# Adding the shared part of a routed feed-forward block onto scattered rows by accumulating stores

## The chip, the cores and the metric

The kernel runs on one core of a Trainium2 chip. The metric is device time in microseconds (us). Engine names are those of the profile: PE multiplies matrices (PEld is its weight load), DVE, ACT and POOL work on tiles, SP only issues transfers. PE writes to banks of PSUM; everything else lives in on-chip tiles or in device memory (names that end in `_dram`, the inputs `in_...`, and the result `out`).

## The reference

For 4096 tokens (2 sequences of 2048) of width 256, in 32-bit floats, the result is a sum of four parts:

```python
xn  = layernorm(x)
out = x + attention(xn) + (xn + moe(layernorm(xn, ln_w, ln_b)))
```

`attention` is a causal linear attention with 16 heads of 16 channels: queries and keys are expanded into Chebyshev polynomials up to order 5, prefix sums run over the tokens, and a numerator is divided by a denominator before the output projection. `moe` is the feed-forward block:

```python
logits  = xf @ router_w                       # 8 experts
top_idx = argmax(logits); top_score = sigmoid(max(logits))
routed  = for each token, with expert e = top_idx and xe = xf * top_score:
              (silu(xe @ gate_w[e]) * (xe @ up_w[e])) @ down_w[e]
shared  = (silu(xf @ sh_gate) * (xf @ sh_up)) @ sh_down
moe     = routed + shared
```

Each token goes to exactly one expert, so each row of the result gets exactly one routed row.

## The kernel before

The 4096 tokens are cut into 8 chunks of 512 tokens (`NC`, index `c`), each of 4 tiles of 128 rows (`NT`, index `t`). One on-chip tile per chunk, `X[c]` with 128 partitions x 4 x 256, first holds the input rows, then `x + xn`, and then takes the results of the attention and of the shared experts by additions on DVE: `accumulate` (L958) adds two row tiles at a time from a PSUM bank; for the very last pair, chunk 7's tiles 2 and 3, L949 adds one tile at a time.

Routed experts work on sorted tokens. `route` computes for 34 slot tiles (`NJ`) of 128 rows which token sits in which row: `take_i` and `give_i`. `expert(n, j)` loads the weights of the expert of slot tile `j` on SP's queue, gathers its 128 rows by an indirect transfer on POOL's queue (L1183), multiplies (L1201 for gate and up, L1222 for down), copies the result from PSUM to a tile `yt` (L1225 on ACT or L1226 on DVE), and scatters `yt` by an indirect transfer on POOL's queue (L1229) to the rows `give_i` of the scratch tensor `y_dram`; padding rows have an index out of bounds and are left out. Each scatter is recorded in `y_ins`.

When all 34 scatters have landed, the last loop of the kernel (L1247 on) combines the two halves. For each chunk SP loads 512 KB of `y_dram` into a free weight buffer (L1251; the load has explicit dependencies on all instructions in `y_ins`), DVE adds it to `X[c]` (L1260, one instruction over 128 x 1024), and SP stores `X[c]` to the result (L1264): one transfer of 512 KB per chunk, but for the last chunk 256 KB and twice 128 KB.

The order of instructions on each engine is computed when the program is built: `op` declares an operation with its engine, an assumed cost, what it reads (`r`), writes (`w`) and adds to (`a`), and a priority; `Plan.order` simulates the engines and emits operations as they become ready. The numbers in `op` (0.45, 1.25 and so on) are this planner's assumptions. Each engine then runs its own list in order, and waits on semaphores where data come from elsewhere. The shared experts' last two chunks are held back (`hold`) so that PE computes them at the end, beside and behind the last routed tiles. Combining has the lowest priority (`60 + c`), so it stands last on every queue that it uses.

Of the kernel before, what the change touches and what calls it, by code (L numbers as in the profile page):

```python
# [11 lines left out]
F32 = mybir.dt.float32  # L12
I32 = mybir.dt.int32
AF = mybir.ActivationFunctionType
ALU = mybir.AluOpType
# [3 lines left out]
SP = mybir.EngineType.SP  # L19

P = 128
NB, S, D = 2, 2048, 256
NTOK = NB * S
NH, DH = 16, 16
NE, FF = 8, 512
CH = 512
NT = CH // P
# [11 lines left out]
NJ = NFULL + (NPART + 3) // 4  # L39
# [60 lines left out]
class Plan:  # L100
# [13 lines left out]
    def op(self, eng, cost, emit, r=(), w=(), a=(), prio=0.0, alloc=(), nbytes=None, alt=(), table=None,  # L114
           after=(), grow=None):

        o = Op()
        o.seq, o.prio, o.alloc, o.nbytes, o.table, o.grow = len(self.ops), prio, list(alloc), nbytes, table, grow  # L120
        o.alts = [(eng, cost, emit)] + list(alt)
        need = {}
        for k in r:
            need.update(dict.fromkeys(self.adds.get(k, ())))
            if k in self.last:
                need[self.last[k]] = None
            self.reads.setdefault(k, []).append(o)
        for k in a:
            if k in self.last:
                need[self.last[k]] = None  # L130
            need.update(dict.fromkeys(self.reads.get(k, ())))
            self.adds.setdefault(k, []).append(o)
        for k in w:
            if k in self.last:
                need[self.last[k]] = None
            need.update(dict.fromkeys(self.reads.get(k, ())))
            need.update(dict.fromkeys(self.adds.get(k, ())))
            self.last[k], self.reads[k], self.adds[k] = o, [], []
        need.pop(o, None)
        o.soon = [n for n in after if n not in need]  # L140
        need.update(dict.fromkeys(after))
        o.need, o.after, o.done = need, [], None
        o.bufs = {}
        for k in tuple(r) + tuple(w) + tuple(a):
            b = k[0] if isinstance(k, tuple) else k
            if isinstance(b, Buf):
                o.bufs[b] = None
        for b in o.alloc:
            b.owner = o
        for b in o.bufs:  # L150
            b.users += 1
            if b.owner is not o:
                need[b.owner] = None
        self.ops.append(o)
        return o
# [100 lines left out]
def kernel(  # L256
# [19 lines left out]
    dram = ctx.enter_context(tc.tile_pool(name="dram", bufs=1, space=DRAM))  # L276
# [2 lines left out]
    ctx.enter_context(tc.manual_schedule())  # L279

    z_dram = dram.tile([NTOK, D], F32, name="z_dram")
    y_dram = dram.tile([NTOK, D], F32, name="y_dram")
    ratio_dram = dram.tile([NTT, P], F32, name="ratio_dram")
    xn_dram = [dram.tile([P, KD, CH], F32, name=f"xn_dram_{c}") for c in range(NC)]
    xf_dram = [dram.tile([P, KD, CH], F32, name=f"xf_dram_{c}") for c in range(NC)]
# [37 lines left out]
    give_i = const.tile([P, NJ], I32, name="give_i")  # L323
# [3 lines left out]
    X = [const.tile([P, NT, D], F32, name=f"X_{c}") for c in range(NC)]  # L327
# [27 lines left out]
    w_p = Pool([big[:, i * 1024 : (i + 1) * 1024] for i in range(NW)])  # L355
# [15 lines left out]
    op = plan.op  # L371
    V, A, G, S_, T_ = nc.vector, nc.scalar, nc.gpsimd, nc.sync, nc.tensor
    MM, M256, MT = 0.86, 0.442, 0.115
    KiB = 1024
# [13 lines left out]
    for c in range(NC):  # L388
        if c == 0:
            for t in range(NT):  # L390
                op("SP", 0.45, lambda t=t: S_.dma_start(out=X[0][:, t, :], in_=x[ts(t, P)]),
                   w=[("X", 0, t)], nbytes=128 * KiB, prio=-90)
# [7 lines left out]
                out=rw[:, :, NE * (GP - 1) : NE * GP], in_=router_w.rearrange("(k p) e -> p k e", p=P)), w=["rw"], nbytes=64 * KiB, prio=-88.5)  # L400
            op("SP", 0.45, lambda: S_.dma_start(out=sg, in_=sh_gate.rearrange("(k p) f -> p k f", p=P)),
               w=["sg"], nbytes=512 * KiB, prio=-88)
            op("SP", 0.45, lambda: S_.dma_start(out=su, in_=sh_up.rearrange("(k p) f -> p k f", p=P)),
               w=["su"], nbytes=512 * KiB, prio=-87)
        else:
            op("SP", 0.45, lambda c=c: S_.dma_start(
                out=X[c], in_=x[c * CH : (c + 1) * CH].rearrange("(t p) d -> p t d", p=P)),
               w=[("X", c, t) for t in range(NT)] + [("x_in", c)], nbytes=512 * KiB, prio=-80 + 5 * c)
        if c == 1:
            op("SP", 0.45, lambda: S_.dma_start(out=sd, in_=sh_down.rearrange("(k p) d -> p k d", p=P)),  # L410
               w=["sd"], nbytes=512 * KiB, prio=-73)
            op("SP", 0.45, lambda: S_.dma_start(out=w_in, in_=w_in_t.rearrange("(k p) e -> p k e", p=P)),
               w=["w_in"], nbytes=768 * KiB, prio=-74)
        if c == 2:
            op("SP", 0.45, lambda: S_.dma_start(out=w_out, in_=w_out_t.rearrange("(k p) e -> p k e", p=P)),
               w=["w_out"], nbytes=256 * KiB, prio=-68)
# [18 lines left out]
    def stat(c, tiles=range(NT), behind=()):  # L435
        for t in tiles:
            i = c * NT + t

            def f(c=c, t=t, i=i):
                V.bn_stats(stats[:, i, :], X[c][:, t, :])  # L440
                V.bn_aggr(mv[:, i, :], stats[:, i, :])

            op("DVE", 0.58, f, r=[("X", c, t)], w=[("mv", i)], prio=FRONT + 0.1 * c - 0.15,
               after=evicted + list(behind))
# [50 lines left out]
    def front(c):  # L495
# [7 lines left out]
        for t in range(NT):  # L503
            i = c * NT + t

            def f(t=t, i=i):
                V.tensor_scalar(zall[:, i, :], X[c][:, t, :], mv[:, i, 0:1], rs[:, 1, i : i + 1],
                                ALU.subtract, ALU.mult)

            def f_(t=t, i=i):  # L510
                A.activation(zall[:, i, :], X[c][:, t, :], AF.Identity,
                             bias=nm[:, 2, i : i + 1], scale=rs[:, 1, i : i + 1])
            if c:
                op("ACT", 0.59, f_, r=[("X", c, t), ("r", part(c, t)), ("nm", part(c, t))], w=[("z", i)], prio=p,
                   alt=[("DVE", 0.36, f)])
            else:
                op("DVE", 0.36, f, r=[("X", c, t), ("r", part(c, t))], w=[("z", i)], prio=p - 0.37 + 0.1 * (t // HT))
# [107 lines left out]
    for cs in ([0], [1], [2, 3], [4, 5, 6, 7]):  # L625
# [4 lines left out]
        else:  # L630
            for c in cs:
                stat(c)
            a, b = cs[0] * NT, (cs[-1] + 1) * NT
# [502 lines left out]
    for g in range(KD):  # L1136
        b = Buf(T_p, f"W_{g}")
# [5 lines left out]
    for i in range(2):  # L1143
        b = Buf(xfT_p, f"V_{i}")
# [3 lines left out]
    for i, (q, n) in enumerate(((zt_p, D), (sl_p, FF), (hm_p, FF), (yt_p, D))):  # L1148
        b = Buf(tv_p, f"U_{i}")
# [5 lines left out]
    y_ins, downs, ups = [], [], []  # L1155

    def expert(n, j):
# [15 lines left out]
        for n, src, cost in ((0, gate_w, 0.85), (1, up_w, 0.45), (2, down_w, 0.45)):  # L1173
            for i, (h, _) in enumerate(parts):
                def f(h=h, i=i, n=n, src=src, b=sets[i][n]):
                    if n == 0:
                        ev.append(nc.values_load(expert_i[0:1, h : h + 1], engines=[SP], min_val=0, max_val=NE - 1))
                    S_.dma_start(out=b.t.rearrange("p (k f) -> p k f", k=KF if n == 2 else KD),
                                 in_=src[ds(ev[i], 1)].rearrange("o (k p) f -> p (o k) f", p=P))
                downs.append(op("SP", cost, f, r=["experts"] + [("z_dram", n) for n in range(NC)], w=[sets[i][n]],  # L1180
                                alloc=[sets[i][n]], nbytes=512 * KiB, prio=EXQ + e, after=downs[-1:]))

        op("POOL", 1.28, lambda: G.indirect_dma_start(  # L1183
            out=zt.t, out_offset=None, in_=z_dram,
# [4 lines left out]
        def f():  # L1189
            for k in range(KD):  # L1190
                T_.transpose(pz.t[:, ts(k, P)], zt.t[:, ts(k, P)], ident)  # L1191
        op("PE", 2 * MT, f, r=[zt], w=[pz], alloc=[pz, xT], prio=EXQ + e)
        for k in range(KD):
            op("ACT", 0.46, lambda k=k: A.activation(
# [3 lines left out]
        def mm(b, wts_):  # L1198
# [9 lines left out]
           prio=EXQ, table="silu")  # L1208
        op("DVE", 0.75, lambda: V.scalar_tensor_tensor(sl.t, pu.t, sc(), sl.t, ALU.mult, ALU.mult),  # L1209
           r=[pu, zt, sl], w=[sl], prio=EXQ)  # L1210
# [16 lines left out]

        def f():
            y_ins.append(G.indirect_dma_start(  # L1229
                out=y_dram, out_offset=bass.IndirectOffsetOnAxis(ap=give_i[:, j : j + 1], axis=0),  # L1230
                in_=yt.t, in_offset=None, bounds_check=NTOK - 1, oob_is_err=False,
            ).ins)
        op("POOL", 1.28, f, r=[yt, "table"], w=[("y", j)], nbytes=128 * KiB, prio=SCAT)
# [10 lines left out]
        gate = [shared(c, gate + ([hold[c]] if c in hold else spilled if c > 1 else []))]  # L1244


    for c in range(NC):  # L1247
        b = Buf(w_p, f"y_{c}")

        def f(c=c, b=b):  # L1250
            ins = S_.dma_start(  # L1251
                out=b.t.rearrange("p (t d) -> p t d", t=NT),
                in_=y_dram[c * CH : (c + 1) * CH].rearrange("(t p) d -> p t d", p=P),
            ).ins
            for s in y_ins:
                tc.add_manual_dep(ins, s.name, mybir.DependencyInfo(
                    mybir.DependencyClass.Sync, mybir.DependencyReason.DATA))
        op("SP", 0.45, f, r=[("y", j) for j in range(NJ)], w=[b], alloc=[b], nbytes=512 * KiB, prio=60 + c)
        keys = [("X", c, t) for t in range(NT)]
        op("DVE", 1.25, lambda c=c, b=b: V.tensor_tensor(  # L1260
            X[c].rearrange("p t d -> p (t d)"), X[c].rearrange("p t d -> p (t d)"), b.t, ALU.add),
           r=[b], a=keys, prio=60 + c)
        for t, n in ((0, 2), (2, 1), (3, 1)) if c == NC - 1 else ((0, NT),):
            op("SP", 0.45, lambda c=c, t=t, n=n: S_.dma_start(  # L1264
                out=out[ds(c * CH + t * P, n * P)].rearrange("(t p) d -> p t d", p=P), in_=X[c][:, t : t + n, :]),
               r=keys[t : t + n], w=[("out", c, t)], nbytes=n * 128 * KiB, prio=60 + c)

    for _, _, emit in plan.order():
        emit()
# [37 lines left out]
```

## Time and profile before

| | us |
|---|---|
| median of 3 runs (570.54 to 570.64) | 570.56 |
| profiled execution | 570.69 |
| its span, first to last instruction | 569.0 |
| PE busy | 563.1 (99%) |
| DVE busy | 486.2 (85%) |
| ACT busy | 238.0 (42%) |
| POOL busy | 99.7 (18%) |
| eight adds L1260, mean of one | 1.22 |
| two adds L949, mean of one | 0.42 |

The granted clock of TensorE is full throughout. DMA moved 132.67 MB in the span, a mean of 233 GB/s: 121.65 MB by SP's (hardware) queue, 10.51 MB by POOL's (software) queue. The profile's rows name a line, an engine, an operation and the tiles written and read (`out<-in`); "POOLq" and "SPq" stand for what those engines' sequencers do, such as issuing a transfer. The busy time of an issuing row is the time of issue, not that of the data. Buffers are named by the memory they were cut from: the loads of `y_dram` appear as `T<-y_dram`, `big<-y_dram` and `xfT<-y_dram`. The DMA share in a table by stage is the mean busy share of the 16 DMA engines; it can come out a little over 1.

### The profile page before, as it was taken

The page shows a single profiled execution, that of the slowest core. Times are in us where ns is not written, and L with a number is a line of the kernel's source. Part 1 is how long each engine was busy: PE and PEld are TensorE (multiplying, and loading weights), DVE is VectorE, ACT ScalarE, POOL GpSimd, SP SyncE. Part 2 cuts the span into 40 slices and gives each one's busy share as a digit, 9 for nine tenths or more (in the row PEclk, how much of TensorE's full clock was granted, in tenths as well). Part 3 has the DMA queues.
Part 4 walks back from the last instruction along what each step waited for, and adds up shares of the span by engine and source line. Part 5 has one row for each costly group of instructions (what it writes and reads, how often), then busy time and mean ns, then how long its engine had stood idle before and what let it go on. Part 6 is the DMA issues. An engine that isn't in the chain of part 4 may idle for free.

```text
span 569.0 us, 8176 instructions
## 1 busy us (share of the span) xinstructions
PE 563.1 (99%) x2691; PEld 305.4 (54%) x2691; DVE 486.2 (85%) x799; ACT 238.0 (42%) x469; POOL 99.7 (18%) x113
## 2 busy tenths in 40 slices
PE   8999999999999999999999999999999999999997
PEld 7564555665535555464445455464555644553655
DVE  6899899999999999999899998999999999931254
ACT  4779662012553362354236435424733543311110
POOL 4211000005021102212120322215031321210100
PEclk9999999999999999999999999999999999999999
DMA  8857651336249918893884699299679938991089
GB/s 283 275 164 259 223 222 37 126 123 243 74 141 365 333 47 268 304 352 93 297 288 165 219 348 363 53 353 336 234 224 308 388 106 285 380 373 67 10 271 328
DMA packets 87689, 132.67 MB, mean 233 GB/s; under 512 B 5681, under 2 KB 52063, under 8 KB 87648
## 3 DMA queue, kind: packets, MB, share of 16 engines
q1 hardware_dynamic: 83152, 121.65, 62.7%
q0 software_dynamic: 3952, 10.51, 5.3%
q8 instruction: 21, 0.34, 0.3%
q14 instruction: 20, 0.16, 0.1%
q10 hardware_dynamic: 544, 0.00, 0.1%
HBM read 113.26 MB, written 19.15 MB: 233 GB/s over the span
## 4 chain that ended last, share of the span: by engine, by line
PE 98%; DVE 1%; DMA 0%; ACT 0%; issue 0%; DVEq 0%
PE bank L1201 22%; PE bank L924 20%; PE bank L987 15%; PE bank L1222 11%; PE bank L942 10%; PE bank L1125 5%; PE bank L1214 3%; PE psk L1017 3%; PE psq L1017 3%; PE bank L1191 1%; PE psk L1030 1%; PE bank L554 1%; PE psk L1111 1%; PE bank L874 1%; PE bank L587 1%; PE bank L1098 0%
## 5 line engine op out<-in xcount | busy, mean ns | idle before, releaser
L1201 PE MATMUL bank<-big,wide 128*32 128x512 f32 (+1 forms) x344 | 102.9, 596 | 0.0
L1229 POOL DMA_INDIRECT y_dram<-wide,give_i x32 | 41.4, 1293 | 304.1 <-ACT wide L1225 152.1
L987 PE MATMUL bank<-xnT,w_in 128*128 128x512 f32 x192 | 86.7, 594 | 0.0
L1054 DVE TENSOR_TENSOR_SCAN tv<-ones,carry,tv 128x512 f32<-128x512 f32 x60 | 76.6, 1277 | 1.2
L924 PE MATMUL bank<-xfT,sg 128*128 128x512 f32 (+1 forms) x136 | 61.1, 574 | 1.1 <-ACT xfT L532 1.1
L924 PE MATMUL bank<-xfT,su 128*128 128x512 f32 (+1 forms) x136 | 61.0, 573 | 0.0
L1201 PEld LDWEIGHTS bank<-big,wide 128*32 128x32 f32 (+1 forms) x344 | 34.6, 144 | 45.9 <-issue 42.1
L1183 POOL DMA_INDIRECT wide<-z_dram,take_i x34 | 42.9, 1262 | 85.5 <-DVE give_i L899 72.6
L942 PE MATMUL bank<-sd,hT 128*128 128x256 f32 x256 | 57.5, 379 | 0.0
L987 PEld LDWEIGHTS bank<-xnT,w_in 128*128 128x128 f32 x192 | 35.6, 190 | 39.0 <-issue 35.9
L1222 PE MATMUL bank<-big,wide 128*32 128x256 f32 (+1 forms) x352 | 54.2, 384 | 0.0
L942 PEld LDWEIGHTS bank<-sd,hT 128*128 128x128 f32 x256 | 48.0, 190 | 8.7 <-issue 2.5
L931 ACT ACTIVATE hT<-bank 128x512 f32<-128x512 f32 x32 | 19.0, 596 | 77.7 <-PE bank L924 73.5
L1222 PEld LDWEIGHTS bank<-big,wide 128*32 128x32 f32 (+1 forms) x352 | 37.0, 148 | 19.6 <-issue 7.5
L1207 ACT ACTIVATE wide<-bank,slot_s 128x512 f32<-128x512 f32 x33 | 22.6, 686 | 58.7 <-PE bank L1201 58.6
L1201 PE MATMUL bank<-xfT,wide 128*32 128x512 f32 (+1 forms) x100 | 45.6, 597 | 0.0
L1074 DVE TENSOR_TENSOR o<-o,tv 128x512 f32<-128x512 f32 x64 | 44.2, 690 | 1.7
L1209 DVE SCALAR_TENSOR_TENSOR wide<-bank,slot_s,wide 128x512 f32<-128x512 f32 x33 | 24.5, 743 | 17.9 <-PE bank L1201 17.5
L924 PEld LDWEIGHTS bank<-xfT,sg 128*128 128x128 f32 x136 | 24.6, 190 | 26.8 <-issue 24.1
L924 PEld LDWEIGHTS bank<-xfT,su 128*128 128x128 f32 x136 | 24.6, 190 | 25.3 <-issue 23.8
L1009 DVE SCALAR_TENSOR_TENSOR T<-T 128x1024 f32<-128x1024 f32 x32 | 38.1, 1220 | 0.0
L958 DVE TENSOR_TENSOR X<-X,bank 128x512 f32<-128x512 f32 x31 | 21.1, 679 | 15.6 <-PE bank L942 9.3
(224 smaller groups left out, 859.2 us busy)
## 6 DMA issues: line engine op xcount, KB each, us to landing
big<-in_gate_w SPq DMA_DIRECT2D x45, 512.0 KB
big<-in_down_w SPq DMA_DIRECT2D x44, 512.0 KB
big<-in_up_w SPq DMA_DIRECT2D x41, 512.0 KB
xfT<-in_up_w SPq DMA_DIRECT2D x14, 512.0 KB
xfT<-in_gate_w SPq DMA_DIRECT2D x11, 512.0 KB
xfT<-in_down_w SPq DMA_DIRECT2D x9, 512.0 KB
z_dram<-big SPq DMA_DIRECT2D x8, 512.0 KB
X<-in_x SPq DMA_DIRECT2D x7, 512.0 KB
```

Source lines behind the costliest of these rows:

```text
L924: T_.matmul(b.t[:, cols], wt[:, k, ts(f, P)], vx(k)[:, cols], start=(k == 0), stop=(k == KD - 1))
L942: T_.matmul(po.t[:, ts(i, D)], hT[f].t[:, ts(tp * 2 + i, P)], sd[:, f, :], start=(f == 0), stop=(f == KF - 1))
L987: T_.matmul(pm.t, w_in[:, k, ds(i * D + g * P, P)], xnT.t[:, ts(k, CH)], start=(k == 0), stop=(k == KD - 1))
L1009: op("DVE", 1.27, lambda i=i, j=j, q=part: V.scalar_tensor_tensor(q[i](), q[j](), off[i], q[1](), ALU.subtract, ALU.mult), r=[(T, j)] + X2 ...
L1017: T_.matmul(pt.t[ts(i - 1, QD), :], heads[:, 24 - g * HB : 24 - g * HB + QD], half[i](side), start=(g == 0), stop=(g == KD - 1 and (i > KD ...
L1054: o_ = op("DVE", 1.25, lambda b=b, i=i, g=g: V.tensor_tensor_scan(b.t, ones[:, 0:1].to_broadcast([P, CH]), b.t, 0.0 if opening else old[:, ...
L1074: op("DVE", 0.66, lambda o=o, b=b: V.tensor_tensor(o(), o(), b.t, ALU.add), r=[b, ok], w=[ok], prio=p)
L1125: T_.matmul(pa.t[:, ts(i, D)], o2.t[:, ds(g * CH + (tp * 2 + i) * P, P)], w_out[:, g, :], start=(g == 0), stop=(g == KD - 1))
L1183: op("POOL", 1.28, lambda: G.indirect_dma_start(out=zt.t, out_offset=None, in_=z_dram, in_offset=bass.IndirectOffsetOnAxis(ap=take_i[:, j ...
L1201: T_.matmul(b.t[n, :], xT.t[:, ds(k * P + n.start, n.stop - n.start)], wt.t[:, ts(k, FF)], start=(k == 0), stop=(k == KD - 1), skip_group_ ...
L1222: T_.matmul(py.t[n, :D], hmT.t[:, ds(i * P + n.start, n.stop - n.start)], wd.t[:, ts(i, D)], start=(i == 0), stop=(i == KF - 1), skip_grou ...
L1229: y_ins.append(G.indirect_dma_start(out=y_dram, out_offset=bass.IndirectOffsetOnAxis(ap=give_i[:, j : j + 1], axis=0), in_=yt.t, in_offset ...
```

## The change

The scratch tensor `y_dram` goes. The 34 scatters write the routed rows to the result `out` itself. The loads of `y_dram` on SP and the adds on DVE are gone. The ten stores of `X[c]`, with the same sizes as before, are issued from POOL's queue as accumulating stores: what is in `X[c]` is added to what stands in `out`. Each has explicit dependencies on all 34 scatters. The planner gives them an assumed cost of 1.0 on POOL. The order on PE and ACT stays the same instruction by instruction, and DVE's list differs by the eight adds alone.

```diff
-    y_dram = dram.tile([NTOK, D], F32, name="y_dram")
...
             y_ins.append(G.indirect_dma_start(
-                out=y_dram, out_offset=bass.IndirectOffsetOnAxis(ap=give_i[:, j : j + 1], axis=0),
+                out=out, out_offset=bass.IndirectOffsetOnAxis(ap=give_i[:, j : j + 1], axis=0),
                 in_=yt.t, in_offset=None, bounds_check=NTOK - 1, oob_is_err=False,
             ).ins)
...
     for c in range(NC):
-        b = Buf(w_p, f"y_{c}")
-
-        def f(c=c, b=b):
-            ins = S_.dma_start(
-                out=b.t.rearrange("p (t d) -> p t d", t=NT),
-                in_=y_dram[c * CH : (c + 1) * CH].rearrange("(t p) d -> p t d", p=P),
-            ).ins
-            for s in y_ins:
-                tc.add_manual_dep(ins, s.name, mybir.DependencyInfo(
-                    mybir.DependencyClass.Sync, mybir.DependencyReason.DATA))
-        op("SP", 0.45, f, r=[("y", j) for j in range(NJ)], w=[b], alloc=[b], nbytes=512 * KiB, prio=60 + c)
         keys = [("X", c, t) for t in range(NT)]
-        op("DVE", 1.25, lambda c=c, b=b: V.tensor_tensor(
-            X[c].rearrange("p t d -> p (t d)"), X[c].rearrange("p t d -> p (t d)"), b.t, ALU.add),
-           r=[b], a=keys, prio=60 + c)
         for t, n in ((0, 2), (2, 1), (3, 1)) if c == NC - 1 else ((0, NT),):
-            op("SP", 0.45, lambda c=c, t=t, n=n: S_.dma_start(
-                out=out[ds(c * CH + t * P, n * P)].rearrange("(t p) d -> p t d", p=P), in_=X[c][:, t : t + n, :]),
-               r=keys[t : t + n], w=[("out", c, t)], nbytes=n * 128 * KiB, prio=60 + c)
+            def f(c=c, t=t, n=n):
+                ins = G.dma_start(
+                    out=out[ds(c * CH + t * P, n * P)].rearrange("(t p) d -> p t d", p=P), in_=X[c][:, t : t + n, :],
+                    accum_op=ALU.add).ins
+                for y in y_ins:
+                    tc.add_manual_dep(ins, y.name, mybir.DependencyInfo(
+                        mybir.DependencyClass.Sync, mybir.DependencyReason.DATA))
+            op("POOL", 1.0, f, r=keys[t : t + n] + [("y", j) for j in range(NJ)], w=[("out", c, t)], nbytes=n * 128 * KiB,
+               prio=60 + c)
```

## The prediction

> **What bounds the kernel now.** I began with the page's shares: PE is busy 563.1 of 569.0 us at full granted clock, and the chain that ended last is 98% PE. PE's work is untouched by this change, and so is its order, so the question is the stretch behind PE's last matmul, and whatever could push it out. The end of that chain, in order of time (start, length, what):
>
> ```profile
> 544.66 13.73 PE bank L924 x32
> 558.40 6.92 PE bank L942 x32
> 565.32 0.02 issue
> 565.34 0.42 DVE X L949
> 565.76 0.33 DVEq L1303
> ```
>
> PE runs without a gap to 565.32; then DVE adds the last two row tiles (L949), and 2.9 us after that the span is over. The timeline of those us, all engines and then SP's queue from 520 us on:
>
> ```profile
> 565.34 0.75 DVE L949 TENSOR_TENSOR X<-X,bank 128x256 f32<-128x256 f32 x2 [2.77 <-PE bank L942]
> 565.79 0.83 SPq L1264 DMA_DIRECT2D out<-X  x2
> ...
> 542.57 1.47 SPq L1251 DMA_DIRECT2D T<-y_dram  x3
> ```
>
> SP issues each of the last two 128 KB stores in 0.83 / 2 = 0.42 us, as soon as its tile is added (565.76 and 566.09). The eight loads of y start at 542.57, when the last scatter has landed. Line L1303, the end of the program, says that SP is through with its last waits at 568.1; so 0.9 us of the span is the closing barrier:
>
> ```profile
> L1303 SPq DRAIN  x3: 7/7/7, 568.1 to 568.4; - x3
> ```
>
> The third view is the table by stage over the tail (window, length, busy time of PE, PEld, DVE, ACT, POOL, then clock, DMA share, GB/s):
>
> ```profile
> 552.00:554.00 2.00, 2.00 (x6) 0.82 (x5) 2.00 (x3) 0.60 (x1) 0.00 (x0) 1.00 1.10 349
> ...
> 560.00:562.00 2.00, 2.00 (x11) 1.77 (x10) 0.44 (x2) 0.00 (x0) 0.00 (x0) 1.00 1.09 385
> ...
> 565.00:566.00 1.00, 0.30 (x2) 0.00 (x0) 0.66 (x2) 0.00 (x0) 0.00 (x0) 1.00 1.09 384
> 566.00:567.00 1.00, 0.00 (x0) 0.00 (x0) 0.10 (x1) 0.00 (x0) 0.00 (x0) 1.00 0.72 248
> 567.00:568.00 1.00, 0.00 (x0) 0.00 (x0) 0.00 (x0) 0.00 (x0) 0.00 (x0) 1.00 0.45 149
> ```
>
> This is what the shares hide: from 544 to 566 us the DMA engines are full. They move 348 GB/s while loads of y and stores of X are mixed, 385 GB/s when stores are alone. After 566 us 0.248 + 0.149 = 0.40 MB are left, of which the last two stores are 0.26; so the last stores stand behind 0.14 MB, 0.35 us. PE and the DMA engines finish almost together: a tail with little slack in it.
>
> **The change, part by part.**
>
> *Removed, worth about nothing.* Eight adds of 128x1024 (L1260, 1.22 us each, 9.8 us of DVE). From 500 us on DVE is busy 23.6 of 69 us; the adds that matter for the end (L958 at 561.89, L949 at 565.34) start when PE releases them, with DVE waiting 1.56 and 2.77 us. Cover: PE. Eight loads of y (4.19 MB) and SP's issue of them: SP has nothing else to issue there.
>
> *The scatters* go to the result instead of a scratch tensor: the same 34, with the same waits in the same places of POOL's queue, 128 KB each. Nothing.
>
> *Moved and added: ten accumulating stores on POOL's queue*, behind the last scatter and waiting for all 34. Nothing but themselves is queued behind them, and no other engine waits for POOL any more. They can start where the loads of y started, at 542.6; tiles 0 to 6 are complete at 544.70 + 0.69 = 545.4, before their turn. So seven stores of 512 KB and one of 256 KB (its tiles are ready at 561.89 + 0.69 = 562.6) have until 566 us behind PE, and the last two of 128 KB don't.
>
> *POOL's issue.* The trace has no accumulating store. POOL's nearest rows:
>
> ```profile
> L499 POOL DMA_DIRECT2D wide<-ratio_dram x7 | 3.8, 549 | 9.7 <-DMA ratio_dram<-wide 9.7
> L1229 POOL DMA_INDIRECT y_dram<-tv,give_i x2 | 2.0, 984 | 8.2 <-issue 6.0 <-DMA y_dram<-wide,give_i 2.2
> ...
> y_dram<-tv,give_i POOLq DMA_INDIRECT x2, 2.4
> ```
>
> A direct transfer to 128 partitions takes POOL 0.55 us, an indirect one of 128 rows 0.98. For the last stores (128 rows) I take 0.75 from between these. For 512 rows the floor is 0.55 and the ceiling four times 0.98, 3.9; I take 1.3, nearer to the direct row, since they are direct. The scatter lands 2.4 us from its issue, so 1.42 after POOL is done with it: 128 KB at 385 GB/s are 0.34 of that, and I split the rest (an estimate) in 0.6 until the data flows and 0.5 until it is confirmed.
>
> *The end, if only latency counts.* The last two are issued from 565.8: 565.8 + 2 x 0.75 + 1.42 + 0.34 (a second read of 128 KB) + 0.9 = 570.0; with 0.55 or 0.98 as POOL's price 569.6 or 570.4. Against 569.0 that is +1.0 (+0.6 to +1.4). The Trainium skill (DMA: Bandwidth & Descriptors, Specifications) gives a first byte after about 1 us from POOL's queue and 0.6 from SP's; that alone would make it +0.4, as it counts one transfer and not the two that follow each other on POOL. I keep the rows.
>
> *The transfer rate, which decides.* Before, each byte of y and X cost one read and one write for the load and the same for the store: 8.39 MB read in all. An accumulating store reads X and the row of the result, and writes once: again 8.39 MB read. The row: mixed traffic at 348 GB/s gives 174 GB/s of stored data, 24.1 us for 4.19 MB. The Trainium skill (Collectives: The Full Stack, "The bandwidth ceiling: the fold count and why AG ≠ RS ≠ AR") has a rule that speaks against the idea that adding on the way is free: a reducing transfer takes two source reads on the same ring, and so moves half of what a copy moves (62.28 against 32.35 GB/s there). Half of the 385 of stores alone would be 192, 21.8 us. The measured mix has the reads and writes of memory that an accumulation has, so I start from 174. The other bound: read, read and write of a row one after the other, a third of 348, 116 GB/s, 36.2 us. Near the first, I take off once more the tenth that mixing cost (385 to 348), because these rows alternate between the two within each engine: 157 GB/s, 26.7 us.
>
> *Sum.* 542.6 + 1.3 (first issue) + 0.6 = 544.5 first data; + 26.7 = 571.2; + 0.5 confirmed + 0.9 barrier = 572.6, against 569.0. The median shown is 570.56, 1.56 above the span (this execution itself took 570.69): 572.6 + 1.56 = **574.2 us**. At 174 GB/s the sum is 570.0, equal to the end by latency; each 1 us of transfer beyond that is 1 us of time, for PE no longer hides it.
>
> **Rivals.** About 0.2%, 1.14 us, is what can be told from no change: under 569.4, over 571.7.
>
> *A, the DMA engines drain the sum too slowly* (above): 574.2; with 174 to 116 GB/s, 571.8 to 583.7. For it: they were full before with the same reads.
>
> *B, the other side: the backlog is gone before the last tile.* If two reads and a write overlap so well that at least 174 GB/s are stored, for instance because memory sees 4 MB fewer writes, the seven stores are through by 566 us and the end is POOL's latency alone: 571.1 to 572.0, best 571.4. The point that decides is 24 us for 4.19 MB. Against it: 348 was the best rate of mixed traffic in the same place. Faster than before is nearly excluded: SP's issue was quicker than POOL's, and all that can come back is the 0.35 us of backlog.
>
> *C, POOL's issue is the bound.* 3.9 us per 512 rows: 542.6 + 7 x 3.9 = 569.9, + 1.95 + 0.98 + 0.98 = 573.8, + 1.42 + 0.34 + 0.9 = 576.5, so 578.0. For it: the cost by row of the indirect form; against: the direct form at 549 ns. It decides above 3 us per store.
>
> *D, rows wait for their own round trip.* The scatter shows at most 1.1 us for it (1.42 - 0.34). Each of 16 engines has 256 rows; with one at a time they take 282 us, four deep 70 us: 544.5 + 70 + 1.4 = 616, so 617.5. For it: a read must be back before the add. Against: plain 1 KB rows in this tail run at full rate, so many are in flight.
>
> That the change does nothing can't be: the ten stores do stand on POOL's queue and the adds are gone from DVE's.
>
> **How the numbers follow.** A 0.50, B 0.27, C 0.09, D 0.12, faster than before 0.02. The range: from 571.0, the floor of the latency sum (569.6 + 1.56 = 571.1), to 590, which takes in A's and C's ends and a rate of 97 GB/s (43 us), the start of D; what is left out is most of D and the chance of faster. Within 0.2% lies a good half of B: 0.17. Slower: the rest of B, A, C, D: 0.81. Faster: 0.02.
>
> **What would show it.** PE's last matmul still ends at 565.3 with no gap, and SP's queue is empty in the tail. The table by stage shows DMA full from about 544 to beyond 568, at 300 GB/s or more if written and read bytes both count, or about 160 if only stored ones do. POOL's stores: 512-row issues near 1.3 us (C: near 4), 128-row near 0.75. The end comes 6 to 7 us after L949. I am wrong if DMA has idle time before 565 us (B), if POOL is busy without a break from 542 to 570 (C), or if PE's end has moved.

## The result, and the profile after

The changed kernel takes 576.58 us (576.48 to 576.73, 5 runs) against 570.64 us of the kernel before beside it (570.54 to 571.5, 5 runs): 1.0101 times as long, 95% interval 1.0087 to 1.0116. That is 5.9 us more. The profiled execution's span went from 569.0 to 574.8 us. Slower was forecast, with 574.2 us; what makes it slower is for the most part not what the forecast said.

Line numbers of the changed kernel are one less than before up to the last loop; L1251 is the accumulating store. Its table by stage, in the columns used above:

```profile
546.00:548.00 2.00, 2.00 (x7) 0.80 (x6) 0.00 (x0) 0.60 (x1) 2.00 (x5) 1.00 1.20 190
...
562.00:564.00 2.00, 2.00 (x11) 1.77 (x10) 0.63 (x1) 0.00 (x0) 1.07 (x1) 1.00 1.24 198
564.00:566.00 2.00, 1.36 (x7) 0.85 (x5) 0.60 (x2) 0.00 (x0) 0.11 (x1) 1.00 1.04 117
566.00:568.00 2.00, 0.00 (x0) 0.00 (x0) 0.15 (x1) 0.00 (x0) 1.76 (x2) 1.00 0.69 85
568.00:569.00 1.00, 0.00 (x0) 0.00 (x0) 0.00 (x0) 0.00 (x0) 0.00 (x0) 1.00 1.01 123
569.00:570.00 1.00, 0.00 (x0) 0.00 (x0) 0.00 (x0) 0.00 (x0) 0.00 (x0) 1.00 0.74 105
570.00:571.00 1.00, 0.00 (x0) 0.00 (x0) 0.00 (x0) 0.00 (x0) 0.00 (x0) 0.65 0.00 0
...
573.00:574.00 1.00, 0.00 (x0) 0.00 (x0) 0.00 (x0) 0.00 (x0) 0.00 (x0) 0.50 0.00 0
```

Three things are to be seen. The GB/s count stored bytes alone (over all windows they add up to the 4.19 MB that are stored), and they flow at 177 to 198 GB/s from 546 to 564 us, 193 in the mean. The backlog is gone when the last stores come: by the packets in the trace (the pieces in which the queues move their data), the stores of 512 and 256 KB have ended at 566.9 and the last pair's data begin at 567.6. And from 570 to 574.8 us nothing computes and nothing moves. PE's work ends where it did, at 565.4 (561.74 + 3.62):

```profile
561.74 3.62 PE L941 MATMUL bank<-sd,hT 128*128 128x256 f32 x16
```

What fills the last 4 us is in the rows of the program's last line, for POOL's and SP's sequencers (the part of an engine that reads its instructions). Each row has three instructions: shortest, median and longest in ns, then the first and the last start. First the changed kernel, then POOL's of the kernel before, whose SP row is in the prediction:

```profile
L1295 POOLq DRAIN  x3: 46/109/7371, 566.6 to 574.5; - x3
L1295 SPq DRAIN  x3: 7/7/7, 570.6 to 574.2; - x3
```

```profile
L1303 POOLq DRAIN  x3: 46/103/7733, 539.7 to 568.7; - x3
```

Each engine has a DRAIN instruction on this line before the closing barrier, in which the engines wait for each other. The first of POOL's three takes over 7 us in both kernels. Before, its row began at 539.7, just ahead of the start of the last scatter, and it was over at 539.7 + 7.73 = 547.4, with 18 us of PE's work still to come. Now it comes behind the last accumulating store and ends at 566.6 + 7.37 = 574.0. SP has seen all transfers landed at 570.6 (before: 568.1) and waits for POOL in the barrier. So the 5.8 us of span are 2.5 us by which the last data land later, and 3.4 us by which POOL's drain outlasts them; the barrier after it takes 0.8 us, as it took 0.9 before. This holds for all runs shown here: in the changed kernel and ten of the eleven variants below the span ends 0.81 us after POOL's long drain, and in the two kernels where SP's last wait ends later than that drain (the kernel before, and e9 below), 0.85 us after SP.

The chain of work that ended last does end on POOL, but shows 0.87 us of the drain and not its length; its last two pieces (start, length, what):

```profile
566.12 0.89 POOL out L1251
567.00 0.87 POOLq L1295
```

### The profile page after: what moved, and what is told of

The parts are those of the page before. It is cut to its first block, busy times and chain, and to the rows that moved or that the text cites. A ratio compares the mean times of both kernels' runs of the same rounds, so it can differ in the third digit from the quotient of the medians.

```text
span 574.8 us, 8143 instructions
## 1 busy us (share of the span) xinstructions
PE 563.6 (98%) x2691; PEld 306.0 (53%) x2691; DVE 477.1 (83%) x791; ACT 238.1 (41%) x469; POOL 112.3 (20%) x123
## 5 line engine op out<-in xcount | busy, mean ns | idle before, releaser
L1228 POOL DMA_INDIRECT out<-wide,give_i x32 | 41.2, 1289 | 303.8 <-ACT wide L1224 152.2
L932 DVE TENSOR_TENSOR hT<-hT,bank 128x512 f32<-128x512 f32 x32 | 21.8, 683 | 17.4 <-PE bank L923 17.1
```

What stands on the lines that cost most here:

```text
L1228: y_ins.append(G.indirect_dma_start(out=out, out_offset=bass.IndirectOffsetOnAxis(ap=give_i[:, j : j + 1], axis=0), in_=yt.t, in_offset=No ...
```

## The experiments

**Theory 1** is the drain: the end waits for POOL's closing drain, and the accumulating stores are to blame only as POOL's last work. **Theory 2** is the prediction's: the accumulating transfers are what is late. Four kernels tell them apart. "POOL's data" below is the end of the last data packet of POOL's queue in the trace (569.9 in the changed kernel).

**e1 and e2: part of the tail on its old way.** In e1 the last two row tiles of chunk 7 are loaded, added and stored as before (from the result instead of `y_dram`); in e2 the whole of chunk 7. The core of e2, with the old form in a helper `loaded` and the new one in `accumulated`:

```diff
-    for c in range(NC):
...
+    loaded(NC - 1, 0, NT, ((0, 2), (2, 1), (3, 1)))
+    for c in range(NC - 1):
+        accumulated(c, ((0, NT),))
```

> The changed kernel, but the last two row tiles of chunk 7 go the old way: SP loads their routed rows from the result, DVE adds them, SP stores them plainly. POOL's last accumulating store is that of 256 KB, issued from 562.9 to 564.1. Theory 1 (the end waits for POOL's closing drain, which in the changed kernel ran until 6.1 us after its last issue): drain until 564.1 + 6.1 = 570.2, span about 570.9 to 571.0, time 572.4 to 572.8. Theory 2 (the accumulating transfers themselves are what is late): the tail is SP's again and the engines are no fuller than before, time 570.3 to 571.0.

> The same for all of chunk 7: POOL accumulates chunks 0 to 6 only, its last issue ends near 552. Theory 1: the drain ends near 558, hidden behind PE; the end is SP's stores as before, span 568.6 to 569.1, time 570.2 to 570.7. Theory 2: 3.67 MB are still accumulated at some 196 GB/s until about 563.5 beside a load of 0.5 MB, and the last stores meet what is left of it: 570.4 to 572. If under 570.3, the 0.35 us of backlog in which the last stores of the kernel before stood has been won.

e1: 573.34 us, 1.0044 times before (1.0027 to 1.006). e2: 572.84 us, 1.0034 (1.0021 to 1.0046). The drains, e1's and then e2's, with SP's row of each:

```profile
L1320 POOLq DRAIN  x3: 46/109/8077, 562.8 to 571.4; - x3
L1320 SPq DRAIN  x3: 7/7/7, 568.2 to 571.2; - x3
```

```profile
L1320 POOLq DRAIN  x3: 46/109/23982, 546.4 to 570.9; - x3
L1320 SPq DRAIN  x3: 7/7/7, 568.7 to 570.6; - x3
```

In e1 SP is through at 568.2, as before the change, and the span still ends at 571.7, 0.8 us behind POOL's drain (562.8 + 8.08 = 570.9). Theory 2 fails there. e2 misses what theory 1 said of it: the drain isn't over at 558, 6 us after POOL's last issue (552.0), but at 570.4. POOL's data moved until 566.5: 3.67 MB take 19 us at 193 GB/s, and from 564 us on they shared the engines with SP's stores. So the drain also waits for POOL's own transfers: from their last data to its end it took 4.0 us in the changed kernel, 4.0 in e1 and 3.9 in e2.

**e3: plain stores from POOL.** The changed kernel without the addition; the result lacks the routed rows.

```diff
-                    accum_op=ALU.add).ins
+                    ).ins
```

> The changed kernel with plain instead of accumulating stores from POOL, all else the same; the routed rows are left out of the result (they are overwritten). Theory 1: the last issue ends at 567.0 to 567.9, drain 6.1 us, span 573.9 to 574.8, time 575.4 to 576.5. Theory 2: half of the reads, stores at up to 385 GB/s, done long before 565; time 570.5 to 571.3. The rate of the stores in its tail, beside the 196 GB/s of the accumulating ones, tells what the second read costs.

577.08 us, 1.0109 (1.0092 to 1.0126): as slow as accumulating. Its stages:

```profile
552.00:554.00 2.00, 2.00 (x6) 0.90 (x5) 0.48 (x1) 0.56 (x1) 0.00 (x0) 1.00 1.04 354
554.00:556.00 2.00, 2.00 (x6) 0.94 (x5) 0.69 (x1) 0.04 (x1) 0.00 (x0) 1.00 0.68 242
556.00:558.00 2.00, 2.00 (x6) 0.80 (x6) 0.00 (x0) 0.60 (x1) 0.00 (x0) 1.00 0.00 0
...
562.00:564.00 2.00, 2.00 (x11) 1.74 (x10) 0.69 (x1) 0.00 (x0) 0.71 (x1) 1.00 0.00 0
...
568.00:569.00 1.00, 0.00 (x0) 0.00 (x0) 0.00 (x0) 0.00 (x0) 0.00 (x0) 1.00 0.27 94
```

```profile
L1295 POOLq DRAIN  x3: 46/109/7962, 566.7 to 575.2; - x3
L1295 SPq DRAIN  x3: 7/7/7, 569.1 to 574.9; - x3
```

The seven big stores are done by 556, and the DMA engines stand idle until the next store is issued: there is no backlog at all. The end is 6.4 us later than before. The data land 1.0 us later than before (569.1 against 568.1), the drain is over at 574.7. This also gives the price of accumulating: 354 GB/s at best here against 198. The packets differ in size as well: 4 KB and 191 ns each in e3, or 48 ns per KB, against 1 KB and 102 ns in the changed kernel. The size alone doesn't explain it: the plain 1 KB packets of SP's stores in the kernel before took 46 ns.

**e4: one plain store on POOL.** The kernel before, its very last 128 KB store moved:

```diff
+            e, d = ("POOL", G) if (c, t) == (NC - 1, 3) else ("SP", S_)
-            op("SP", 0.45, lambda c=c, t=t, n=n: S_.dma_start(
+            op(e, 0.45, lambda c=c, t=t, n=n, d=d: d.dma_start(
```

> The kernel before with a single edit: the very last store (128 KB, chunk 7 tile 3, plain) is issued from POOL's queue. Theory 1: issue 566.1 to 566.7, drain until 572.8, span 573.5, time 575 to 575.3. Theory 2: a plain transfer of 128 KB that starts some tenths later, 570.7 to 571.3.

576.16 us, 1.0093 (1.0076 to 1.011). POOL's drain:

```profile
L1304 POOLq DRAIN  x3: 46/109/7248, 566.5 to 574.3; - x3
L1304 SPq DRAIN  x3: 7/7/7, 569.2 to 574.0; - x3
```

It ends at 573.8; SP was through at 569.2. One transfer out of ten on POOL's queue, not even an accumulating one, has nearly the price of the whole change.

e1, e3 and e4 came out 0.5 to 0.9 us above the range that theory 1 had given. It took the drain's end as 6.1 us behind POOL's last issue, as in the changed kernel; in these three it was 6.9, 7.3 and 6.6 us.

**e5 and e10: no transfer, a copy of 128 numbers.** The kernel before, and on POOL a copy of one column of the last tile, behind everything (e5), or of chunk 7's first tile, which is complete 3.5 us earlier (e10):

```diff
     for _, _, emit in plan.order():
         emit()
+    G.tensor_copy(sqb[:, 0:1], X[NC - 1][:, NT - 1, 0:1])
```

> The kernel before, and behind everything on POOL's queue one copy of 128x1 that reads what the last add wrote (its target is a constant no longer used). No transfer of POOL's is near: its last one landed at 542.4. Theory 1a (the long closing drain belongs to POOL's transfers, and comes out at their last data plus 4 to 6 us): the drain is over within 0.3 us of the copy, at about 566.6, and the time is that of before, 570.5 to 570.9. Theory 1b (POOL's drain is long after any work of POOL): drain until about 572.5, time 574 to 575.5.

> The kernel before with the 128x1 copy on POOL again, but on chunk 7's first row tile, which is complete at 562.6 instead of 566.1. If the drain is a length of 6.5 us from POOL's last instruction: copy at 562.7 to 562.9, drain until 569.4, span 570.2, time 571.6 to 572. If it were bound to the end of the whole program instead (to SP's or DVE's end), 575.4 as with the late copy.

e5: 575.41 us, 1.0082 (1.0062 to 1.0102). Theory 1b holds, not 1a. POOL's timeline and its drain:

```profile
566.17 0.18 POOL L1270 COPY sqb<-X 128x1 f32<-128x1 f32 x1 [25.24 <-DVE X L949]
```

```profile
L1304 POOLq DRAIN  x3: 46/103/6753, 566.1 to 573.4; - x3
L1304 SPq DRAIN  x3: 7/7/7, 568.1 to 573.2; - x3
```

POOL's own transfers had been over for 24 us, SP is through at 568.1 as before, and the drain still lasts 6.5 us from the copy's end (566.35 to 572.9). This is the cleanest proof: 4.7 us of time for 0.18 us of work, with no transfer touched. e10 gave 571.91 us (571.84 to 572.0), 1.0019 (1.0011 to 1.0027), inside what was expected:

```profile
L1304 POOLq DRAIN  x3: 46/103/6755, 562.6 to 569.9; - x3
```

The drain is over at 569.4, again 6.5 us behind the copy's end (562.84). In that profile SP itself was through only at 569.2, so e10 shows the drain's length, and its time alone would not convict the drain.

**e6: enter the drain after the landing.** The changed kernel, and behind it on POOL a write to the tile of the last store, which has to wait until that has landed:

```diff
+    G.memset(X[NC - 1][:, NT - 1, 0:1], 0.0)
```

> The changed kernel, and behind the last accumulating store POOL zeroes one column of the tile that it stored, so POOL waits until that store has landed (near 570.3) before it comes to its drain. Theory 1a with the drain counted from the last data: 570 + 4 = 574.0 again, time 576.3 to 577. If the drain only repeats a wait for the landing that is now over: drain at 570.6, span 571.3, time 572.9 to 573.3. If the drain takes a length of its own from when it is entered: 570.5 + 4 to 6, time 577 to 579.

577.44 us, 1.0118 (1.0098 to 1.0138).

```profile
L1296 POOLq DRAIN  x3: 46/109/4339, 571.0 to 575.8; - x3
```

The drain began at 571.0, when POOL's data had been through since 570.6, and still took 4.3 us: it has a length of its own and doesn't merely repeat the wait for the landing. (Between 4.2 us here and 6.5 in e5, counted from POOL's last instruction, something sets the length that these runs don't show.)

**e8: the last two stores joined.**

```diff
-        for t, n in ((0, 2), (2, 1), (3, 1)) if c == NC - 1 else ((0, NT),):
+        for t, n in ((0, 2), (2, 2)) if c == NC - 1 else ((0, NT),):
```

> The changed kernel with the last two 128 KB stores joined to one of 256 KB: one issue of 1.2 us from 566.2 instead of two of 0.9 and 1.2 in a row. If the price of the end is POOL's serial issue of small stores, the data end about 0.5 us earlier than at 569.9 and the time is 575.9 to 576.3, the drain still 4 us behind the data. If the engines need the same 2.3 us for these 256 rows from when they are asked, 576.4 to 577.

576.75 us, 1.0106 (1.0085 to 1.0126): no gain. One issue saved didn't bring the end forward; the data end at 570.4 and the drain 4.0 us later.

**e7, e9 and e11: accumulate less, and early.** Chunks 0 to 3 (e7), or 0 and 1 (e9, and e11, in which POOL waits for SP's last load) are accumulated by POOL, the others go the old way. In the helpers of e2, e9 and then what e11 adds:

```diff
+    for c in range(2, NC):
+        loaded(c, 0, NT, ((0, 2), (2, 1), (3, 1)) if c == NC - 1 else ((0, NT),))
+    for c in range(2):
+        accumulated(c, ((0, NT),))
...
-                for y in y_ins:
+                for y in y_ins + loads[-1:]:
```

> Chunks 0 to 3 are accumulated by POOL, chunks 4 to 7 go the old way with their routed rows loaded from the result. If POOL's last data move by 564.2, the drain (4 us later) is hidden and the end is SP's: span 568.7 to 569.2, time 570.3 to 570.9, equal to before. If the shared engines let them end as late as 566, 570.8 + 1.6 = 572.4.

> Chunks 0 and 1 alone are accumulated by POOL (1.05 MB), chunks 2 to 7 go the old way. If POOL's data are through by 564, its drain is hidden, SP ends as before, and the time is 570.4 to 571.0: then nothing of the accumulating store itself costs time, only its place at the end. If POOL's share of the full engines is so small that its data still end at 566, drain until 570, 572 to 572.5 as with four chunks.

> As with two accumulated chunks before, but POOL's two accumulating stores wait until SP's last load of routed rows has landed, so no load is slowed and DVE's adds don't hold up the products behind them. Loads end near 553; POOL's 1.05 MB then share the engines with SP's stores. If POOL's data are through by about 562, drain by 566 to 568, hidden: span 568.8 to 569.2, time 570.4 to 570.9, no difference from before, so the accumulating store costs nothing away from the end. If its data last until 566 as with four and seven chunks, 572 to 572.5. If something else of the accumulating store cost time, more than 570.9 with the drain over before 568.

e7: 572.44 us, 1.0034 (1.002 to 1.0049). e11: 572.12 us, 1.0024 (1.0014 to 1.0033). In e7 POOL's and SP's stores shared the engines evenly (119 GB/s each from 549 to 564 us, by the packets), and POOL's data lasted until 566.1. In e11 POOL's two stores, issued by 557.5, moved no data before 559.8, when SP's earlier stores were through. Then they had the engines nearly to themselves, at 197 GB/s, until 565.8. Two of e11's stages:

```profile
558.00:560.00 2.00, 2.00 (x10) 1.58 (x9) 0.69 (x1) 0.00 (x0) 0.00 (x0) 1.00 1.09 383
...
562.00:564.00 2.00, 2.00 (x11) 1.77 (x10) 0.64 (x1) 0.00 (x0) 0.00 (x0) 1.00 1.24 197
```

The drains end 3.8 and 3.7 us behind the data, at 569.9 and 569.6, outlasting SP again (569.0 and 568.4). So fewer stores from POOL didn't bring its end forward here: SP's transfers kept it late.

e9 got POOL's drain out of the way (560.8), and yet took 573.82 us, 1.0053 (1.0036 to 1.007), for another reason. Parts of its timeline (this profiled execution took 575.3 us, the other three 573.8):

```profile
556.22 1.22 DVE L1275 TENSOR_TENSOR X<-X,big 128x1024 f32<-128x1024 f32 x1 [2.58 <-DMA big<-out]
...
559.72 0.68 DVE L932 TENSOR_TENSOR hT<-hT,bank 128x512 f32<-128x512 f32 x1
...
560.31 1.22 DVE L1275 TENSOR_TENSOR X<-X,big 128x1024 f32<-128x1024 f32 x1
...
560.45 0.70 PE L941 MATMUL bank<-sd,hT 128*128 128x256 f32 x2 [1.15 <-DVE hT L932]
...
562.19 7.52 PE L941 MATMUL bank<-sd,hT 128*128 128x256 f32 x26 [1.03 <-DVE hT L932]
```

The loads of routed rows shared the engines with POOL's stores and came late. The adds (L1275) waited for them on DVE, once for 2.58 us, and the shared experts' products (L932) stood behind the adds. Then PE waited for those, 1.15 and 1.03 us, and worked at a granted clock of 0.53 just after (562 to 564 us). e11 removes that, and is the fairest trial of early accumulation; it is still 1.4 us slower than before. Nothing that was run beats the kernel before.

## Why the prediction was right or wrong

Right in its sign and its range, wrong in its cause. That 574.2 us came within 2.4 us of the measured time is luck: two errors cancel in part. The sum had 2.6 us too many in the transfers (572.6 of span, where its own sum by latency was 570.0), and lacked 1.5 us of landing and 3.4 us of POOL's drain.

*The removed work was worth nothing*: confirmed. PE ends at 565.4, and the adds gone from DVE only lengthen its waits.

*The transfer rate, "which decides"*: this step failed. The sum took 157 GB/s, with 174 as the better end; measured were 193 over 546 to 564 us and 198 in the clean stretches. The Trainium skill's rule of two source reads (Collectives: The Full Stack, "The bandwidth ceiling: the fold count and why AG ≠ RS ≠ AR"), by which adding moves half of what copying moves, gave an estimate of 192 from the 385 of SP's plain stores; that was nearer than the mixed row from which I started. The page states it for collectives; that the second read is the reason here too, no run shows. Taking off a tenth "once more" had no row behind it. At the measured rate the seven stores and the 256 KB are through before the last pair's data start, which was the point where rival B takes over. So A is false, and e3 has the same late end without any backlog. B was right about the transfers, and its 571.1 to 572.0 us still falls 4.6 us short, since it too leaves out the drain. D, which would have begun at 97 GB/s, is out. (By the same sum, A at 174 GB/s is 571.6, not 571.8, and the best of B 571.5, not 571.4; neither changes the argument.)

*The end, if only latency counts*: right in kind, mis-sized. Predicted +1.0 us, measured +2.5 until SP has seen everything landed (570.6 against 568.1). POOL's timeline gives the parts:

```profile
562.93 1.18 POOL L1251 DMA_DIRECT2D out<-X  x1 [10.98 <-DVE X L957]
566.11 1.76 POOL L1251 DMA_DIRECT2D out<-X  x2 [2.01 <-DVE X L948]
```

It begins at 566.1 instead of 565.8, the two issues take 1.76 us instead of 1.5, and SP has seen the last one land 2.7 us after them (570.6 - 567.9), where 1.42 + 0.34 had been taken. The last two stores ran at 105 to 123 GB/s while their data moved (568 to 570 us), not at the rate of the big ones. The price of 1.3 us for 512 rows on POOL was right: seven were issued in 9.2 us, and C is out.

*What was not in the sum*: the drain of POOL at the end, +3.4 us. I read SP's row of the program's last line and took 0.9 us as "the closing barrier"; POOL's row stood beside it, with 7733 ns. It was hidden since it began at 539.7. The prediction even said of the stores that "Nothing but themselves is queued behind them, and no other engine waits for POOL any more": POOL's own end is queued behind them, and SP waits for it in the barrier. e4 and e5 show that this makes most of the difference, with one plain store (+5.45 us) or with a copy of 128 numbers (+4.7 us).

The trace of before had the length too. POOL's last instruction there:

```profile
539.94 0.98 POOL L1229 DMA_INDIRECT y_dram<-tv,give_i  x1 [2.19 <-DMA y_dram<-wide,give_i]
```

It ends at 540.9 and the drain at 547.4, 6.5 us later, the same 6.5 as in e5 and e10. Put behind the last issue as the prediction had it, at 565.8 + 1.5 = 567.3, it gives 567.3 + 6.5 + 0.9 = 574.7 us of span; 574.8 was measured. So near a hit is in part chance: the last issue ended at 567.9, and the drain 6.1 us later. What stays open is what the drain does in its 4 to 6.5 us, and why it is shorter behind accumulating stores.

## What to carry to other kernels

Ask of every engine what its last instruction is, not only of the one that bounds the kernel: before moving work to the end of a queue that had long been idle, look at what that engine does between its last instruction and the closing barrier, and count it from the new place. A saving in bytes and instructions under the cover of a busy engine was worth nothing here, while 0.2 us of work on the wrong engine in the last microseconds cost 4.7 us. Where transfers filled the engines up to the end, a queue with few of them still finished late (e7, e11).

## What the runs showed of the hardware that I had not expected

- POOL's drain at the end of the program was over 3.7 to 6.5 us after the later of its last instruction and its last data: 6.5 after a 0.18 us copy (e5, e10), 5.5 and 6.2 after the last data of plain stores (e4, e3), 3.7 to 4.0 after those of accumulating ones; in e6, 4.2 after its last instruction. The first drains of DVE, ACT and PE were over before 567 us in the changed kernel.
- Accumulating stores of 1 KB rows ran at 198 GB/s of stored data, 0.56 of the 354 that plain stores from the same queue reached. A row occupied an engine for 102 ns, 2.2 times the 46 ns of the same row in SP's plain stores of the kernel before.
- Stores on POOL's queue that met engines kept full by SP's transfers ended late. Four accumulating stores shared the engines evenly with SP's, at 119 GB/s each, and moved until 566.1 (e7); two, issued by 557.5 us, began to move only at 559.8, behind SP's earlier stores (e11).
